# A hand-ordered selective scan: the order of GpSimd's products and of the sums behind them

## The chip, the cores and the metric

The kernel runs on one core of a Trainium2 chip. The metric is the device time of one execution in microseconds (us); of several executions the median is given.

## The reference

Four layers work on an image batch x of shape (4, 64, 64, 96) in float32. Layer 0 is group norm, an input projection to 192 channels and a gate, a 3x3 convolution, and a selective scan with 16 states per channel in four directions. Layers 1 to 3 are a convolution, linear attention with a quantised feed-forward network, and a Fourier filter with a second feed-forward network. The part that matters here is the scan:

```python
def step(h, inp):
    u_t, dt_t, B_t, C_t = inp
    dA = jnp.exp(dt_t[..., None] * A)
    h = dA * h + (dt_t * u_t)[..., None] * B_t[:, None, :]
    y = jnp.sum(h * C_t[:, None, :], axis=-1)
    return (h, y)
```

It is run over the 4096 positions of each image by rows and by columns, and each of these forwards and backwards; the four results are added.

## The kernel before

**Phases and steps.** The scans go over 4 images and 24 groups of 8 channels. 8 channels times 16 states fill the 128 partitions. Each pair of image and group (a unit u) has two phases, n = 2u by rows and n = 2u + 1 by columns, 192 phases in all. The 4096 positions are four chunks q of 1024. A phase has 8 steps, each with one scan instruction on VectorE (DVE): steps 0 to 3 go forward over q = 0 to 3 (L1970), steps 4 to 7 go backward over q = 3 to 0 (L1977). Below, "step 9" of a phase is step 1 of the next.

**What each engine does in a phase.** ScalarE (ACT) makes the decay factors `pa` with an exponential (`decay`, L1669 by rows, L1675 by columns, two instructions there) into PSUM. `B` holds dt·u, multiplied by the replicated B_t on GpSimd (POOL) by `times_b` (L1653). For a column phase ACT copies it in turned order into the single tile `Bc` (`copy_b`, L1628). The forward scan writes `S`. The backward scan writes over `pa`, and DVE then adds that to `S` (L1988); for the chunks in `apart[n]` it writes over `B` or `Bc` instead, and forward and backward results stay apart. POOL multiplies each result by the replicated C_t (`times_c`, L1658). TensorE (PE) sums over the 16 states (`reduce`, two blocks of a chunk, L1691) into the PSUM tile `py`, which collects a whole unit. ACT copies `py` to `ys` (`result`, L1698), and SyncE (SP) stores it.

**Two stages.** While images 1 to 3 are still being prepared (projection, convolution, softplus: the "pre" part of the main lane), only chunk 3 stays apart: three adds on DVE and five products on POOL per phase. When `done["pre"]` is set, chunks 2 and 3 stay apart: two adds, six products.

**The S tiles.** There are five. `places` says which tile chunk q of phase n takes: q = 1 takes the tile that q = 2 of the phase before had, q = 2 that of q = 3, q = 3 that of q = 1, and q = 0 that of q = 0 two phases before. A forward scan can start once the sum over the old content is done. `B` has four tiles: chunk q of the next unit takes the tile of chunk q ^ 1 of this one. `Bc` has one.

**What sets the order.** The part runs under a manual schedule, so each engine executes its instructions in the order in which the program issues them. `plan(n)` puts the loads, copies, products and sums of a phase at chosen steps with `at(t + k, ...)`, where t = 8n. After the instructions of a step, `pieces(step)` fills in side work: the "pre" part and layers 1 to 3 of images 0 to 2 (the main lane), and the gating and output projection behind the scans (the side lane). Side work is cut into pieces with a cost for each of PE, ACT, POOL, DVE and DMA; every step adds `gains[step]` to five credits (step counted to 16, a row and a column phase), a piece is issued when the credits cover it, and `cap` bounds what can be saved up. What is left over after the last scan is issued in the tail, before the last layers of image 3.

Of the kernel before, what the change touches and what calls it, by code (L numbers as in the profile page):

```python
# [73 lines left out]
def layers(ctx: ExitStack, tc: tile.TileContext, a: dict, out):  # L74
# [37 lines left out]
    late = []  # L112
# [22 lines left out]
    done = {}  # L135
# [1446 lines left out]
    def phase(n):  # L1582

        b, g = units[n // 2]
        return b, g, n % 2
# [130 lines left out]
    class Lane:  # L1716
# [32 lines left out]
    credit = [0.0] * 5  # L1749

    gains = [
        (2.8, 1.2, 0.4, 0.8, 1.6), (2.8, 1.2, 0.4, 0.8, 1.6),
        (2.8, 0.2, 0.4, 0.8, 1.6), (2.8, 0.4, 2.2, 0.8, 1.6),
        (2.8, 1.2, 0, 0.8, 1.6), (2.8, 1.4, 0.4, 0.8, 1.6),
        (3.2, 1.0, 1.2, 1, 1.8), (3.2, 2.4, 1.4, 1, 1.8),
        (2.8, 1.4, 0.4, 0.8, 1.6), (2.8, 1.4, 0.4, 0.8, 1.6),
        (2.8, 1.4, 0.4, 0.8, 1.6), (2.8, 2.4, 0.6, 0.8, 1.6),
        (2.8, 2.8, 0.6, 0.8, 1.6), (2.8, 1.4, 0.6, 0.8, 1.6),
        (3.2, 2.4, 0.8, 1, 1.8), (3.2, 2.4, 1.4, 1, 1.8),
    ]  # L1760
    cap = (4.4, 3.0, 3.2, 1.6, 4.0)

    def pieces(step):

        clock[0] += 1
        assert clock[0] % 16 == (step + 1) % 16
        for free, bank in returned:
            free.append(bank)
        returned.clear()
        for e in range(5):  # L1770

            more = 1.25 if e in (2, 4) and clock[0] > 8 * (N - NG) else 1
            credit[e] = min(cap[e], credit[e] + gains[step][e] * more)
        for lane in list(lanes):
            if not lane.live():
                lanes.remove(lane)
                continue
            for s in list(lane.streams):
                while s[1] is not None:
                    if s[1] == NEXT:  # L1780
                        if s[2] == clock[0]:
                            break
                        lane.advance(s)
                        continue
                    if s[1] == LONG:
                        if step != 12:
                            break
                        cost = (0, 5.0, 0, 0)
                    else:
                        cost = s[1]  # L1790
                        if any(
                            c > 0 and credit[e] < min(c, cap[e]) - 0.5 for e, c in enumerate(cost)
                        ):
                            break
                    for e in range(len(cost)):
                        credit[e] -= cost[e]
                    lane.advance(s)
                if s[1] is None:
                    lane.streams.remove(s)
# [88 lines left out]
    def at(step, f, *args):  # L1888
        acts.setdefault(step, []).append((f, args))

    def plan(n):

        t, u = 8 * n, n // 2
        two = "pre" in done
        apart[n] = (3, 2) if two else (3,)
        row = n % 2 == 0
        b, g, _ = phase(n)
        last, first = g == NG - 1, g == 0

        if row:  # L1900
            for q, k in ((0, 7), (1, 8), (2, 9), (3, 10)):
                at(t + k, load_du, u + 1, q)
            for q, k in ((0, 3), (1, 5), (2, 15), (3, 16)):
                at(t + k, load_delta, u + 1, q)
            if last:
                for q in range(NCH):
                    at(t + 2 + q, load_rep, b + 1, 0, q)
                for q, k in ((3, 8), (2, 9), (1, 11), (0, 12)):
                    at(t + k, load_rep, b + 1, 1, q)
            for q, k in ((2, 2), (3, 3), (1, 4), (0, 6)):  # L1910
                at(t + k, copy_b, u, q)
            if first:
                for q in range(NCH):
                    at(t + 6 + q // 2, copy_rep, b, q)
        else:
            for q, k in ((0, 2), (1, 3), (2, 6), (3, 9)):
                at(t + k, times_b, u + 1, q)

        if two:
            at(t + 4, times_c, n, 2)  # L1920
            at(t + 5, times_c, n, 3)
            at(t + 6, times_c, n, 3, True)
            at(t + 7, times_c, n, 2, True)
            at(t + 6, reduce, n, 2)
            at(t + 7, reduce, n, 3)
            at(t + 8, reduce, n, 3, True)
            at(t + 8, reduce, n, 2, True)
        else:
            at(t + 4, times_c, n, 3)
            at(t + 6, times_c, n, 3, True)  # L1930
            at(t + 7, times_c, n, 2)
            at(t + 6, reduce, n, 3)
            at(t + 8, reduce, n, 3, True)
            at(t + 8, reduce, n, 2)
        late = 0 if row else 1
        at(t + 8, times_c, n, 1)
        at(t + 9 + late, times_c, n, 0)
        at(t + 10, reduce, n, 1)
        at(t + 10 + 2 * late, reduce, n, 0)
        if not row:  # L1940
            at(t + 13, result, u)
            for j in range(4):
                at(t + 14 + j, store_result, u, j)

    with tc.manual_schedule():
# [4 lines left out]
        for step in range(8 * N):  # L1950
            n, k = divmod(step, 8)
            if k == 0:
                plan(n)
                if n % (2 * NG) == 2 * NG - 2 and n // 2 + 1 < len(units):
                    b = units[n // 2 + 1][0]
                    assert done.get(("back", b)) == NBLK, (n, done)
# [10 lines left out]
            if k < 4:  # L1967
                q = k
# [5 lines left out]
            else:  # L1974
                q = 7 - k
# [8 lines left out]
                else:  # L1984
                    if q:
                        edge = big.tile([128, 1], F32, tag="edge", name="edge", bufs=2)
                        nc.vector.tensor_copy(edge, to[:, 0:1])
                    nc.vector.tensor_tensor(Ss[n, q], Ss[n, q], to, ALU.add)  # L1988
            pieces(step % 16)
            if n == N - 1 and k >= 4:  # L1990
                for i in (2 * k - 8, 2 * k - 7):
# [24 lines left out]
def kernel_body(tc: tile.TileContext, a: dict, out):  # L2016
    layers(tc, a, out)
# [117 lines left out]
```

## Time and profile before

| | |
|---|---|
| median of 3 runs | 5522.77 us (5522.01 to 5528.18) |
| profiled execution | 5537.81 us |
| its span | 5536.0 us |
| busy PE / DVE / ACT / POOL | 77% / 83% / 64% / 72% of the span |
| scan 128x1024 on DVE | 2.28 us first of a row, 2.35 us others |
| product 128x1024 on POOL | 2.36 us, 1481 in all |
| add on DVE (L1988) | 1.22 us, 439 in all |
| copy into columns on ACT | 1.98 us, 384 in all |

The span is the time from the first to the last instruction in the trace; 1.8 us of the execution lie around it. The profiled execution is 15 us above the median of the others. The scans run from 299 to 5103 us. DVE's share counts only instructions, so a wait between two scans shows as idle time, and each row of the page says which engine's instruction ended it.

### The profile page before, as it was taken

The numbers are of one execution on the slowest core, as the hardware profiler recorded it, in microseconds if no ns is written. First come the engines' busy times: TensorE is split into PE (matmuls) and PEld (weight loads), VectorE is DVE, ScalarE is ACT, GpSimd is POOL, SyncE is SP. The second block draws the span as 40 slices with busy tenths as digits, with TensorE's granted clock in tenths as the row PEclk, the third lists the DMA queues.
The fourth block names the chain that finished last, engine by engine and source line by source line (L and its number), as shares of the span: only waits on it lengthen the run. The fifth ranks groups of instructions, "written<-read, shape, count | busy, mean of one in ns | idle before, by whom it ended". The sixth has DMA issues, their size and how long they took to land. (4 is left out here: it accounts for less than half of the span.)

```text
span 5536.0 us, 60837 instructions
## 1 busy us (share of the span) xinstructions
PE 4258.0 (77%) x20550; PEld 1581.5 (29%) x20550; DVE 4618.4 (83%) x3098; ACT 3566.0 (64%) x4554; POOL 3973.4 (72%) x1968
## 2 busy tenths in 40 slices
PE   7967888878886876777658876877578767786878
PEld 4422222222221221345102211542012213451346
DVE  4268888788889998999899999999898989998454
ACT  5667777777786568666865677576755676566133
POOL 1357877778778778878887788787987787787000
PEclk9977989888997986678668866787588768886888
DMA  4334444434456533455456434363565335563012
GB/s 125 91 110 115 126 114 117 135 105 124 117 162 175 163 99 89 128 160 156 125 145 173 117 87 119 115 200 103 147 170 146 97 99 165 161 176 96 17 55 96
DMA packets 298092, 694.68 MB, mean 125 GB/s; under 512 B 58184, under 2 KB 95156, under 8 KB 297652
## 3 DMA queue, kind: packets, MB, share of 16 engines
q1 hardware_dynamic: 297780, 690.80, 44.2%
q8 instruction: 162, 2.65, 0.2%
q14 instruction: 150, 1.23, 0.1%
HBM read 564.22 MB, written 126.35 MB: 125 GB/s over the span
## 5 line engine op out<-in xcount | busy, mean ns | idle before, releaser
L1658 POOL TENSOR_TENSOR S<-S,rep 128x1024 f32<-128x1024 f32 x768 | 1806.5, 2362 | 678.9 <-DVE S L1970 628.4
L1691 PE MATMUL py<-S,red 128*32 128x512 f32 x3072 | 956.8, 782 | 380.9 <-POOL S L1658 273.1
L1675 ACT ACTIVATE pa<-dl,nega 128x512 f32<-128x512 f32 x1152 | 792.9, 689 | 579.0 <-DVE Bc L1977 295.3
L1669 ACT ACTIVATE pa<-dl,nega 128x1024 f32<-128x1024 f32 x576 | 642.2, 1115 | 515.7 <-DVE S L1988 239.5
L1653 POOL TENSOR_TENSOR B<-B,rep 128x1024 f32<-128x1024 f32 x384 | 903.0, 2360 | 14.7 <-DMA B<-du_s 14.7
L1970 DVE TENSOR_TENSOR_SCAN S<-pa,S,Bc 128x1024 f32<-128x1024 f32 x288 | 676.3, 2348 | 230.8 <-PE py L1691 161.2
L1970 DVE TENSOR_TENSOR_SCAN S<-pa,S,B 128x1024 f32<-128x1024 f32 x288 | 675.8, 2347 | 134.0 <-PE py L1691 46.3
L1628 ACT COPY Bc<-B 128x1024 f32<-128x1024 f32 x384 | 741.0, 1982 | 0.0
L1988 DVE TENSOR_TENSOR S<-S,pa 128x1024 f32<-128x1024 f32 x439 | 533.7, 1216 | 6.6
L393 PE MATMUL p_conv<-low,conv_w 128*96 128x512 f32 x864 | 421.7, 639 | 32.0 <-ACT u L405 29.4
L1658 POOL TENSOR_TENSOR B<-B,rep 128x1024 f32<-128x1024 f32 x164 | 388.0, 2370 | 75.1 <-DVE pa L1977 38.8
L1977 DVE TENSOR_TENSOR_SCAN B<-pa,B 128x1024 f32<-128x1024 f32 x164 | 379.1, 2312 | 48.2 <-ACT Bc L1628 41.9
L1658 POOL TENSOR_TENSOR Bc<-Bc,rep 128x1024 f32<-128x1024 f32 x165 | 387.0, 2361 | 5.3 <-DVE pa L1977 4.0
L1977 DVE TENSOR_TENSOR_SCAN Bc<-pa,Bc 128x1024 f32<-128x1024 f32 x165 | 381.8, 2314 | 4.7
L1691 PEld LDWEIGHTS py<-S,red 128*32 128x32 f32 x3072 | 118.7, 121 | 908.9 <-POOL S L1658 518.0
L1234 POOL CAST h<-y 128x1536 fp8e5<-128x1536 f16 x64 | 95.5, 1492 | 312.7 <-ACT y L869 301.3
L1977 DVE TENSOR_TENSOR_SCAN pa<-pa,edge,B 128x1024 f32<-128x1024 f32 x124 | 291.5, 2350 | 2.8 <-ACT pa L1669 2.8
L1977 DVE TENSOR_TENSOR_SCAN pa<-pa,edge,Bc 128x1024 f32<-128x1024 f32 x123 | 289.2, 2351 | 5.2 <-ACT pa L1675 5.2
L1691 PE MATMUL py<-Bc,red 128*32 128x512 f32 x660 | 200.0, 787 | 95.1 <-POOL Bc L1658 95.1
L393 PE MATMUL p_conv<-high,conv_w 64*96 64x512 f32 (+1 forms) x576 | 265.0, 597 | 0.0
L1056 PE MATMUL p_mean<-t,centre 96*96 96x512 f32 x256 | 174.3, 792 | 110.7 <-ACT sq L1048 31.8
L1970 DVE TENSOR_TENSOR_SCAN S<-pa,B 128x1024 f32<-128x1024 f32 x96 | 218.9, 2280 | 23.3 <-ACT pa L1669 23.3
(274 smaller groups left out, 7411.4 us busy)
## 6 DMA issues: line engine op xcount, KB each, us to landing
dl<-delta_s SPq DMA_DIRECT2D x770, 256.0 KB
B<-du_s SPq DMA_DIRECT2D x768, 256.0 KB
z_s<-z SPq DMA_DIRECT2D x48, 512.0 KB
zl<-z_s SPq DMA_DIRECT2D x64, 384.0 KB
side<-y_s SPq DMA_DIRECT2D x112, 192.0 KB
rep<-bc_s SPq DMA_DIRECT2D x64, 256.0 KB
tw<-in_dft SPq DMA_DIRECT2D x64, 256.0 KB
side<-in_xT SPq DMA_DIRECT2D x64, 192.0 KB
```

Source lines behind the costliest of these rows:

```text
L393: nc.tensor.matmul(p, lhsT=conv_w[: src.shape[0], k, oc * C : (oc + 1) * C], rhs=src[:, ky : ky + RPB, kx : kx + HW], start=(k == 0), stop ...
L1056: nc.tensor.matmul(pm, lhsT=centre, rhs=t[:, blk(i)], start=True, stop=True)
L1234: nc.gpsimd.tensor_copy(h, y, saturate=False)
L1628: nc.scalar.copy(dst.rearrange("p (w h) -> p h w", h=HW)[:, q * h : (q + 1) * h, :], src.rearrange("p (h w) -> p h w", w=HW),)
L1653: nc.gpsimd.tensor_tensor(Bs[u, q], Bs[u, q], reps[units[u][0], 0, q], ALU.mult)
L1658: nc.gpsimd.tensor_tensor(t, t, c_of(n, q), ALU.mult)
L1669: nc.scalar.activation(pa, dls[u, q // 2][:, at : at + CH], AF.Exp, scale=scale)
L1675: nc.scalar.activation(to[:, k * HW // 2 : (k + 1) * HW // 2, :], src[:, :, q * w : (q + 1) * w], AF.Exp, scale=scale,)
L1691: nc.tensor.matmul(py[32 * j : 32 * j + 32, :], lhsT=red[:, 24 - 8 * s : 56 - 8 * s], rhs=x[:, k * BLK : (k + 1) * BLK], start=s == 0 and ...
L1970: nc.vector.tensor_tensor_scan(s, pas[q], b_of(n, q), Ss[n, q - 1][:, CH - 1 : CH] if q else 0.0, ALU.mult, ALU.add,)
L1977: nc.vector.tensor_tensor_scan(to[:, ::-1], pas[q][:, ::-1], b_of(n, q)[:, ::-1], edge if q < 3 else 0.0, ALU.mult, ALU.add,)
L1988: nc.vector.tensor_tensor(Ss[n, q], Ss[n, q], to, ALU.add)
```

## The change

The change moves issue places; no instruction of the computation is added to a phase or removed from it.

- `plan`: products and sums now come from one list of (chunk, backward or not, step of the product, step of the sum). In the first stage the order on POOL was S3, backward 3, S2, S1, S0 at steps 4, 6, 7, 8, 9 (10 in a column phase) with the sums at 6, 8, 8, 10, 10 (12); it is now S3, S2, backward 3, S1, S0 at 4, 6, 7, 8, 9 (11) with the sums at 6, 7, 8, 9, 10 (12). In the second stage the products keep their steps, apart from S0 of a column phase (10 to 11); the sums of S3, backward 3 and S1 move from 7, 8, 10 to 6, 7, 9.
- `copy_b`: chunk 3 is copied at step 2 and chunk 2 at step 3, instead of the other way round.
- `times_b` of chunk 2 moves from step 6 to 5 of a column phase in the first stage.
- `gains`: other credits for POOL and ACT at the steps; in the first stage PE's are multiplied by 0.9, ACT's by 1.05 and POOL's by 1.25.

```diff
     gains = [
+        (2.8, 0.8, 0, 0.8, 1.6), (2.8, 0.6, 0, 0.8, 1.6),
+        (2.8, 0, 2.2, 0.8, 1.6), (2.8, 0, 0.4, 0.8, 1.6),
         (2.8, 1.2, 0.4, 0.8, 1.6), (2.8, 1.2, 0.4, 0.8, 1.6),
-        (2.8, 0.2, 0.4, 0.8, 1.6), (2.8, 0.4, 2.2, 0.8, 1.6),
-        (2.8, 1.2, 0, 0.8, 1.6), (2.8, 1.4, 0.4, 0.8, 1.6),
-        (3.2, 1.0, 1.2, 1, 1.8), (3.2, 2.4, 1.4, 1, 1.8),
-        (2.8, 1.4, 0.4, 0.8, 1.6), (2.8, 1.4, 0.4, 0.8, 1.6),
-        (2.8, 1.4, 0.4, 0.8, 1.6), (2.8, 2.4, 0.6, 0.8, 1.6),
-        (2.8, 2.8, 0.6, 0.8, 1.6), (2.8, 1.4, 0.6, 0.8, 1.6),
-        (3.2, 2.4, 0.8, 1, 1.8), (3.2, 2.4, 1.4, 1, 1.8),
+        (3.2, 1.0, 1.2, 1, 1.8), (3.2, 2.4, 1.2, 1, 1.8),
+        (2.8, 1.4, 0.2, 0.8, 1.6), (2.8, 1.4, 0.2, 0.8, 1.6),
+        (2.8, 1.4, 0.2, 0.8, 1.6), (2.8, 2.4, 0.2, 0.8, 1.6),
+        (2.8, 2.8, 0.2, 0.8, 1.6), (2.8, 1.4, 0.2, 0.8, 1.6),
+        (3.2, 2.4, 0.6, 1, 1.8), (3.2, 2.4, 1.2, 1, 1.8),
     ]
...
             more = 1.25 if e in (2, 4) and clock[0] > 8 * (N - NG) else 1
+            if "pre" not in done:
+                more = (0.9, 1.05, 1.25, 1, 1)[e]
...
-            for q, k in ((2, 2), (3, 3), (1, 4), (0, 6)):
+            for q, k in ((3, 2), (2, 3), (1, 4), (0, 6)):
                 at(t + k, copy_b, u, q)
...
-            for q, k in ((0, 2), (1, 3), (2, 6), (3, 9)):
+            for q, k in ((0, 2), (1, 3), (2, 6 if two else 5), (3, 9)):
                 at(t + k, times_b, u + 1, q)
 
         if two:
-            at(t + 4, times_c, n, 2)
-            at(t + 5, times_c, n, 3)
-            at(t + 6, times_c, n, 3, True)
-            at(t + 7, times_c, n, 2, True)
-            at(t + 6, reduce, n, 2)
-            at(t + 7, reduce, n, 3)
-            at(t + 8, reduce, n, 3, True)
-            at(t + 8, reduce, n, 2, True)
+            order = ((2, False, 4, 6), (3, False, 5, 6), (3, True, 6, 7), (2, True, 7, 8))
         else:
-            at(t + 4, times_c, n, 3)
-            at(t + 6, times_c, n, 3, True)
-            at(t + 7, times_c, n, 2)
-            at(t + 6, reduce, n, 3)
-            at(t + 8, reduce, n, 3, True)
-            at(t + 8, reduce, n, 2)
-        late = 0 if row else 1
-        at(t + 8, times_c, n, 1)
-        at(t + 9 + late, times_c, n, 0)
-        at(t + 10, reduce, n, 1)
-        at(t + 10 + 2 * late, reduce, n, 0)
+            order = ((3, False, 4, 6), (2, False, 6, 7), (3, True, 7, 8))
+        end = (0, False, 9, 10) if row else (0, False, 11, 12)
+        for q, back, k, r in (*order, (1, False, 8, 9), end):
+            at(t + k, times_c, n, q, back)
+            at(t + r, reduce, n, q, back)
```

## The prediction

> **What bounds the kernel now.** I first read the page's busy shares and slices: VectorE (DVE) is busiest, and the column DVE in the 40 slices goes from 7 or 8 to 9 about a third of the way in. So the scans are cut in two by the number of reverse scans that are kept apart. The page has 439 adds at L1988; 192 phases need two each and a first-stage phase a third, so 439 - 384 = 55 phases belong to the first stage (three adds, five POOL products), and 137 to the second (two adds, six products). I then asked the busy time in each stage (columns: stretch, its length, then PE, PEld, DVE, ACT, POOL busy, clock, DMA).
>
> ```profile
> 298.60:1774.00 1475.40, 1191.73 (x3054) 346.40 (x3054) 1224.95 (x720) 1100.17 (x1396) 1139.50 (x602) 0.85 0.45 126
> 1774.00:5103.00 3329.00, 2462.76 (x13412) 909.67 (x13410) 3092.07 (x1835) 2165.97 (x2689) 2706.96 (x1243) 0.77 0.48 135
> ```
>
> DVE is 83% busy in the first stage (idle 250 us) and 93% in the second (idle 237 us). A pair of phases takes 1475.4 / 27.5 = 53.7 us in the first stage; DVE's own rows give 2 x 2.28 + 6 x 2.35 + 2 x 2.31 + 6 x 2.35 for the scans, 6 x 1.22 for the adds and 4 x 0.16 for the edges, 45.3 us, and about 26 gaps of 0.04 us: 46.3 us. So 7 us of each pair are waits. The waits of DVE say for what, first in the stretch to 1740 us, then 1740 to 4400 us (us, times, longest):
>
> ```profile
> DVE S L1970 <- PE py L1691: 150.1, 33, 7.5
> DVE B L1977 <- ACT Bc L1628: 14.6, 16, 1.1
> ...
> DVE S L1970 <- PE py L1691: 39.8, 25, 4.3
> DVE S L1970 <- ACT pa L1675: 21.8, 24, 2.6
> DVE B L1977 <- ACT Bc L1628: 18.4, 19, 2.6
> ```
>
> A forward scan waits for the sum over states (PE, L1691) that frees its S tile. Counting scans through DVE's timeline places the first-stage waits: 115.1 us in 21 waits at step 1 of a column phase (S of q=1, whose tile held q=2 of the row phase before), 9.4 us at step 1 of a row phase, 36 us at step 3 of both (the tile of the last phase's q=1). One of the 21, in the timelines of DVE, POOL and PE (start, us, operation; idle before it in brackets):
>
> ```profile
> 1302.51 2.28 DVE L1970 TENSOR_TENSOR_SCAN S<-pa,Bc 128x1024 f32<-128x1024 f32 x1
> 1312.32 4.80 DVE L1970 TENSOR_TENSOR_SCAN S<-pa,S,Bc 128x1024 f32<-128x1024 f32 x2 [7.53 <-PE py L1691]
> ...
> 1297.85 2.36 POOL L1658 TENSOR_TENSOR S<-S,rep 128x1024 f32<-128x1024 f32 x1
> ...
> 1294.76 8.43 PE L393 MATMUL p_conv<-low,conv_w 128*96 128x512 f32 x12 [1.27 <-ACT u L405]
> 1303.12 1.05 PE L1691 MATMUL py<-S,red 128*32 128x512 f32 x4
> 1304.10 1.09 PE L544 MATMUL p_dt<-xd,dt_w 6*96 6x512 f32 x2
> 1305.12 2.82 PE L393 MATMUL p_conv<-low,conv_w 128*96 128x512 f32 x6
> 1307.78 0.70 PE L330 MATMUL p_xp<-xb,w_twice 96*128 96x320 f32 x2
> ```
>
> The last line's operation is followed by more convolution; the sum of q=2 begins at 1311.00, beside the backward sum. The product had ended at 1300.2: the scan does not wait for work that is late, but for a sum that is queued behind others on PE.
>
> **What the skill says.** The Trainium skill, "PSUM — Partial Sum Buffer", section "Engine vs sequencer instructions", has ACT, DVE and POOL as strict FIFOs and matmuls in program order; the 10.8 us between that product and its sum agree. So where a sum stands in PE's order decides. "SBUF — State Buffer", section "Who interferes with whom", has a DVE instruction with two SBUF inputs contend with POOL's reads. The adds and scans here read one side from PSUM (pa), and POOL's products last 2362 ns on average, those on the tile B between 2.33 and 2.53 us; I price no contention for their new order. "TensorE: Matmul & The Clock Gate", section "What's actually happening", lets PE's clock follow how busy it was. The trace has 0.85 where PE is 81% busy and 0.77 where it is 74%; I price no change of clock.
>
> **The change part by part.**
>
> (1) Order of products and sums, first stage. The sum of q=2 stood at step 8, after the backward sum; it now stands at step 7, before it, and its product at 6 instead of 7. Its scan is at step 9, so there are two steps instead of one. From the two programs' orders on PE: between the sum of q=0 and this one stood on average 5.0 other matmuls, the sum of q=3, 6.6 more, and the backward sum; now 2.8, the sum of q=3 and 4.3. That is 4.5 matmuls fewer (each has two records; 12 records in the 7 to 8.4 us of a convolution give 1.2 us each), 5.4 us, and one sum of 1.05 us: 6.5 us sooner. The 21 waits average 5.5 us, the longest 7.5: about 110 of 115 us go, and all 9 us of row step 1. Moving the sum of q=1 from step 10 to 9 takes about half of the 36 us at step 3: 18. The POOL step of q=2 comes right after DVE's add at step 5, which is in time; what is behind it on POOL are the backward product and the softplus operations, which had idle before them.
>
> (2) The copies into columns (L1628) take q=3 first; the reverse scan of q=3 at step 4 then waits for the first copy, not the second. The copy is 1.98 us and the waits are 0.9 us: 15 us in the first stage, and most of the 26 us in the second. The scan of q=2 one step later then waits for the second copy, which has a step of 2.3 us to spare.
>
> Together 110 + 9 + 18 + 15 = 152 us of DVE's waits, 5.5 us per pair, to 48.2. **What is late next** is PE. It is busy 1191.7 / 27.5 = 43.3 us of each pair and idle 10.3. Its work is the same in kind and amount (17.9 matmuls of others per pair before, 17.5 after). Its idle time waits mostly for ACT's evacuations: 192 us are named to 1740 us, 7.7 per pair. With DVE faster some of this closes. If half of the 10.3 stays, a pair takes 48.5; if all 7.7 stay, 51.0. I take 6.2: 49.5, or 4.1 us less per pair, 27.5 x 4.1 = **-114 us**.
>
> (3) Second stage. Each phase's sums of q=3, backward q=3 and q=1 stand one step earlier. The waits on sums are 40 + 7 us up to the end, of which I take 30 (one more step is 2.3 us, the mean wait 1.6), and 18 of the copies' 18 + 8. A third comes back as waits on the decays on ACT (the row of 21.8): **-32 us**. Ends: -48, and plus what the rival below gives.
>
> (4) The planner's credits. PE's are cut to 0.9 in the first stage and ACT's raised to 1.05; POOL's are cut at the steps with a product. No instruction of the computation goes. The order of the changed program has 441 adds: the first stage has 57 phases. Two phases with one more add (1.22) and edge (0.16) each: **+3 us**. In the tail, about three blocks of the third image's last feed-forward are left over after the last scan: three plus three matmuls each, some 3 us of PE. A part falls into the 8.5 and 2.6 us for which PE waits for transfers there: **+6 us** (0 to 10).
>
> (5) One times_b (q=2, first stage) goes a step earlier, four steps after its load was issued instead of five. The load is a 256 KB transfer with over 9 us for it; POOL waited for such loads 14.7 us in the whole run. Nothing. The loads on SP keep their steps; the tile that the load at step 9 overwrites is still freed at step 8 or earlier. Nothing.
>
> Sum: -114 - 32 + 3 + 6 = -137. The profiled execution took 5537.8 us (span 5536.0), 15 us above the median of 5522.8; against its own time the sum gives 5401, against the median **5386 us**. About 0.2% (11 us) is what a measurement can tell from no change.
>
> **The rivals.**
> - PE becomes the bound of the first stage: all 7.7 us of waits on ACT stay and the second stage gives nothing. -73 + 9 = -64: 5459. For it: ACT is 75% busy and in order, and its copies stand in bursts at row steps 2 to 6, as before. Against it: ACT itself waits for DVE there (43 + 28 + 16 + 13 us from 600 to 1740 us).
> - All named waits go and nothing replaces them: -152 - 48 + 9 = -191: 5332. Against it: PE would have to be 90% busy (43.3 of 48.2 us).
> - Slower: sums a step earlier stop PE's queue. In the second stage PE already waits for POOL's products before a sum (186.0, 80.2 and 24.5 us for S, Bc and B from 1740 to 4400 us). A sum that stands nearer to its product holds the matmuls of the side work behind it; ACT, in order, then waits for those with the next decay behind. If DVE loses one decay (1.115 us) in each of 137 phases, +153: -114 + 9 + 153 = +48: 5571. It decides from (114 - 9) / 137 = 0.77 us per phase. Against it: PE is 26% idle there.
> - The change does not do what it says, for ACT's decays are as late as the sums, and each wait changes its name: 5523.
>
> **How the numbers follow.** Chances: the sum above 0.56 (its own range 5350 to 5430), PE bound 0.20, all waits gone 0.12, slower 0.08, names only 0.04. So faster 0.88, same 0.04, slower 0.08. From 5335 to 5480 leaves out about half of the third case, the slower one and the names: 2 in 10.
>
> **What would show it.** Right: 441 adds at L1988's place; the wait of the forward scans for py under 60 us in all; first-stage pairs near 49 to 50 us; PE busier than 85% there; the copies' wait under 15 us. Step (3) is wrong if DVE's waits on the decays grow by over 30 us; step (4) if the time from the last scan to the end grows by over 10 us. Wrong in all: waits for py remain at column step 1, or PE's idle per pair is still about 10 us.

## Result and profile after

The changed kernel takes 5563.74 us (median of 5 runs, 5551.78 to 5568.46) against 5528.18 us for the kernel before in the same session: ratio 1.0062, interval 1.0046 to 1.0078. It is slower, by 36 us, where 5386 us was forecast. The profiled execution took 5556.72 us, its span is 5554.8; the two spans differ by only 19 us, because the profiled execution of before lies above its median and that of after below.

The busy time in each stage of the changed kernel (columns as before: stretch, length, then PE, PEld, DVE, ACT, POOL busy, clock, DMA share, GB/s; the third line is the tail after the last scan):

```profile
290.60:1840.00 1549.40, 1312.19 (x3108) 365.31 (x3109) 1274.43 (x751) 1123.30 (x1420) 1173.03 (x616) 0.85 0.44 124
1840.00:5109.10 3269.10, 2448.60 (x13321) 907.63 (x13319) 3046.52 (x1802) 2131.92 (x2637) 2663.04 (x1223) 0.77 0.49 135
5109.10:5554.80 445.70, 358.14 (x3307) 200.54 (x3305) 218.68 (x328) 126.42 (x217) 52.76 (x54) 0.85 0.19 61
```

The page has 441 adds, so 57 phases are in the first stage and 135 in the second. A first-stage pair takes 1549.4 / 28.5 = 54.4 us; it took 53.7 and was to take 49.5. PE is busy 1312.2 / 28.5 = 46.0 us of it (43.3 before) and idle 8.3 (10.3 before). Each number of a stage here and below comes from one profiled execution. Such an execution lies up to 15 us from the median of its kernel, so differences between stages of that size decide nothing by themselves. The second stage takes 24.22 us per phase (24.31 before), the tail 445.7 us (430.4).

The spans' 19 us: the first scan starts 8 us earlier, in code that is the same in both. The first stage is 73 us longer. Two more phases at the second stage's pace account for 48.6; the other 24.6 are the slower pace. The second stage is 62 us shorter, 13 us more than its two missing phases. The tail is 15 us longer.

The waits of DVE, first stage and then second stage (us, times, longest):

```profile
DVE S L1959 <- PE py L1691: 86.5, 31, 4.6
DVE S L1959 <- ACT pa L1669: 75.8, 44, 23.2
DVE pa L1966 <- ACT pa L1675: 38.1, 19, 4.0
DVE S L1959 <- ACT pa L1675: 30.8, 20, 3.9
```

```profile
DVE S L1959 <- ACT pa L1675: 34.7, 39, 3.9
DVE pa L1966 <- ACT pa L1669: 27.5, 22, 2.6
...
DVE S L1959 <- PE py L1691: 5.6, 6, 2.1
```

The wait for sums did fall: from 160 to 86 us over the whole first stage, from 47 to 6 in the second. The copies into columns no longer stand among the first rows. But the decays on ACT stand in their place: their first-stage rows L1669 and L1675 for S were 25.8 and 7.0 us in the same stretch before (23 us of the first is the first scan in both kernels). Here is the place that the prediction showed, a column phase's step 1, in the changed kernel, on PE and then on DVE:

```profile
1443.63 1.92 PE L1691 MATMUL py<-S,red 128*32 128x512 f32 x4 [6.21 <-ACT ys L1698]
1445.48 2.02 PE L544 MATMUL p_dt<-xd,dt_w 6*96 6x512 f32 x2
1448.01 8.05 PE L393 MATMUL p_conv<-low,conv_w 128*96 128x512 f32 x12 [0.51 <-ACT u L405]
1455.99 1.05 PE L1691 MATMUL py<-S,red 128*32 128x512 f32 x4
1456.97 2.82 PE L393 MATMUL p_conv<-low,conv_w 128*96 128x512 f32 x6
1459.71 1.05 PE L1691 MATMUL py<-B,red 128*32 128x512 f32 x4
```

```profile
1457.26 4.80 DVE L1959 TENSOR_TENSOR_SCAN S<-pa,S,Bc 128x1024 f32<-128x1024 f32 x2 [4.02 <-PE py L1691]
```

The sum that frees the tile (1455.99) still comes 4 us late, although it now stands before the backward sum. PE stood still for 6.2 us ahead of it, waiting for ACT's copy of `py`, and then its matmuls took almost twice their time: 1.92 us for a sum that elsewhere takes 1.05, 2.02 us for a p_dt that elsewhere takes 1.09. Each sum now stands by itself. Before, two sums often stood side by side. In the timeline of the kernel before, the place of the prediction goes on so:

```profile
1310.99 0.62 PE L1691 MATMUL py<-B,red 128*32 128x512 f32 x2
1311.00 0.62 PE L1691 MATMUL py<-S,red 128*32 128x512 f32 x2
1311.44 0.60 PE L1691 MATMUL py<-B,red 128*32 128x512 f32 x2
1311.45 0.60 PE L1691 MATMUL py<-S,red 128*32 128x512 f32 x2
...
1314.73 1.06 PE L1691 MATMUL py<-S,red 128*32 128x512 f32 x8
```

Two sums in a row overlap in time: 8 records in 1.06 us, as long as 4 take alone. A sum is two matmuls, and each writes 32 of the 128 partitions of `py`: those of q = 0 and q = 2 the lower half, those of q = 1 and q = 3 the upper. Neighbours that write different halves run together. Neighbours that write the same half do not, as a forward and a backward sum of q = 3 in the second stage show (14 of the 15 such pairs in the kernel before run one after the other):

```profile
2135.07 1.05 PE L1691 MATMUL py<-S,red 128*32 128x512 f32 x4
2135.95 1.03 PE L1691 MATMUL py<-Bc,red 128*32 128x512 f32 x4
```

The Trainium skill, "TensorE: Matmul & The Clock Gate", Part 3, "Packing small matmuls — row/col tiling", describes how matmuls in different 32x32 tiles of the array run at the same time. Here two sums do so only when they stand next to each other in PE's queue. The new order took the neighbours apart. In PE's program order of the first stage, 95 of 275 sums stood directly behind another sum; now 40 of 285 do. Below, such a sum is said to have a neighbour. PE's time in sums (columns: stretch, length, PE, PEld, clock, DMA share, GB/s), before and then after:

```profile
298.60:1774.80 1476.20, 246.29 (x1096) 31.51 (x1096) 0.85 0.45 126
```

```profile
290.60:1840.00 1549.40, 347.33 (x1132) 43.80 (x1132) 0.85 0.44 124
```

That is 9.0 us of PE per pair before and 12.2 after, for the same sums; the clock is 0.85 in both.

### The profile page after: what moved, and what is told of

Read it like the earlier page. It is cut to its first block, busy times and chain, and to the rows that moved or that the text cites. A ratio compares the mean times of both kernels' runs of the same rounds, so it can differ in the third digit from the quotient of the medians.

```text
span 5554.8 us, 60794 instructions
## 1 busy us (share of the span) xinstructions
PE 4365.4 (79%) x20542; PEld 1597.5 (29%) x20542; DVE 4634.1 (83%) x3114; ACT 3563.4 (64%) x4542; POOL 3971.1 (71%) x1966
## 5 line engine op out<-in xcount | busy, mean ns | idle before, releaser
L1675 ACT ACTIVATE pa<-dl,nega 128x512 f32<-128x512 f32 x1152 | 791.1, 689 | 530.6 <-DVE Bc L1966 268.0
L1669 ACT ACTIVATE pa<-dl,nega 128x1024 f32<-128x1024 f32 x576 | 641.9, 1115 | 456.8 <-DVE S L1977 221.9
L1628 ACT COPY Bc<-B 128x1024 f32<-128x1024 f32 x384 | 747.7, 2009 | 16.2 <-POOL B L1653 11.9
L1691 PE MATMUL py<-Bc,red 128*32 128x512 f32 x656 | 231.5, 809 | 104.1 <-POOL Bc L1658 104.0
L1691 PE MATMUL py<-B,red 128*32 128x512 f32 x652 | 204.9, 709 | 61.8 <-POOL B L1658 61.8
L1966 DVE TENSOR_TENSOR_SCAN pa<-pa,B 128x1024 f32<-128x1024 f32 x96 | 226.1, 2356 | 26.3 <-ACT pa L1669 22.6
```

The source lines that it names most:

```text
L1628: nc.scalar.copy(dst.rearrange("p (w h) -> p h w", h=HW)[:, q * h : (q + 1) * h, :], src.rearrange("p (h w) -> p h w", w=HW),)
L1669: nc.scalar.activation(pa, dls[u, q // 2][:, at : at + CH], AF.Exp, scale=scale)
L1675: nc.scalar.activation(to[:, k * HW // 2 : (k + 1) * HW // 2, :], src[:, :, q * w : (q + 1) * w], AF.Exp, scale=scale,)
L1691: nc.tensor.matmul(py[32 * j : 32 * j + 32, :], lhsT=red[:, 24 - 8 * s : 56 - 8 * s], rhs=x[:, k * BLK : (k + 1) * BLK], start=s == 0 and ...
L1966: nc.vector.tensor_tensor_scan(to[:, ::-1], pas[q][:, ::-1], b_of(n, q)[:, ::-1], edge if q < 3 else 0.0, ALU.mult, ALU.add,)
```

## The experiments

Theory A: the sums' lost neighbours make PE's work larger, and that takes back what the slack gives. Theory B: the credits do it, by where side work stands. Theory C: the slack is worth nothing, because another wait follows close behind. (From e9 on the expectations also call it theory C that PE's queue paces the first stage.) The first stage of most of the kernels, per pair ("neighbours": sums directly behind another sum; "sums": PE's time in them):

| kernel | ratio [95%] | phases | pair us | PE busy / idle | sums | neighbours |
|---|---|---|---|---|---|---|
| before | 1 | 55 | 53.7 | 43.3 / 10.3 | 9.0 | 95 |
| after | 1.0062 [1.0046, 1.0078] | 57 | 54.4 | 46.0 / 8.3 | 12.2 | 40 |
| e1 order only | 1.0074 [1.0061, 1.0086] | 55 | 54.4 | 45.3 / 9.1 | 11.1 | 41 |
| e2 credits only | 1.0043 [1.0029, 1.0056] | 57 | 54.4 | 43.9 / 10.5 | 8.9 | 129 |
| e3 joined | 1.0015 [1.0008, 1.0021] | 57 | 53.0 | 43.6 / 9.5 | 9.9 | 77 |
| e4 split | 1.0034 [1.0023, 1.0045] | 55 | 54.5 | 44.3 / 10.2 | 9.7 | 72 |
| e5 joined, two | 0.9993 [0.9984, 1.0001] | 57 | 53.3 | 42.9 / 10.4 | 9.1 | 100 |
| e6 paired | 1.0010 [1.0002, 1.0019] | 55 | 53.5 | 44.0 / 9.5 | 9.5 | 93 |
| e9 before, light | 0.9877 [0.9863, 0.9890] | 55 | 51.4 | 40.9 / 10.5 | 9.7 | 95 |
| e10 after, light | 0.9845 [0.9831, 0.9858] | 57 | 50.6 | 41.6 / 8.9 | 12.2 | 40 |
| e11 paired, light | 0.9881 [0.9866, 0.9896] | 55 | 51.0 | 40.7 / 10.3 | 10.0 | 93 |
| e12 joined, three | 1.0046 [1.0033, 1.0059] | 57 | 54.3 | 42.6 / 11.7 | 8.5 | 124 |
| e13 joined, old credits | 0.9994 [0.9986, 1.0002] | 55 | 53.0 | 43.8 / 9.1 | 9.6 | 87 |
| e14 factors only | 0.9886 [0.9873, 0.9899] | 53 | 51.3 | 43.5 / 7.8 | 10.5 | 130 |
| e15 table only | 1.0068 [1.0056, 1.0080] | 65 | 53.8 | 41.1 / 12.7 | 9.9 | 147 |
| e17 after, old table | 0.9882 [0.9862, 0.9901] | 53 | 50.5 | 43.4 / 7.2 | 11.2 | 96 |
| e18 joined, factors | 0.9839 [0.9821, 0.9857] | 53 | 50.3 | 43.1 / 7.2 | 10.3 | 126 |

**The change in two halves.** e1 is the kernel before with the new order (all hunks of `plan` and `copy_b`), e2 with the new credits (all hunks of `gains` and `pieces`).

> The new order of products, sums and copies with the old credits (gains table and factors of the kernel before). Theory A, lost overlap: in the first stage 95 of 275 sums stood directly behind another sum in PE's order and ran beside it, now 41 do; each sum that runs alone costs PE about 1 us more, and PE is the second bound of the stage. Then the sums' PE time in the first stage is 335 to 345 us (247 before) and the time is still no better than before, 5535 to 5550 us, with the tail after the last scan as before. Theory B, the credits are at fault (side work spread differently, more of it left for the tail): without them the gain of the forecast appears, under 5480 us.

> The old order with the new credits alone. Theory A: the sums keep their neighbours (129 of 285 directly behind another), their PE time in the first stage stays near 250 us, and only the longer tail (about +19 us) and two more first-stage phases (+3 us) cost: 5535 to 5552 us. Theory B: the credits carry the whole loss and hide a gain of the order, so alone they cost over 50 us: above 5580 us.

Measured: 1.0074 (5572.6 us) and 1.0043 (5557.0 us); both cost, and both a little more than theory A had said. With the order alone PE's sums rise from 246 to 305 us (335 were expected at least) and the stage from 1476 to 1496. The waits of DVE in its first stage:

```profile
DVE S L1957 <- ACT pa L1675: 101.3, 36, 5.4
DVE S L1957 <- ACT lg L559: 64.8, 13, 6.0
DVE S L1957 <- ACT pa L1669: 47.9, 22, 23.3
DVE S L1957 <- PE py L1691: 24.7, 10, 6.2
```

So the waits for sums fell by 136 us, from 160 to 25, and the time rose: the scans wait for decays and for `lg`, the logarithm of the softplus on ACT, instead. With the credits alone the sums per pair do not rise; the stage has two more phases and a slower pace, and its granted clock is 0.81. Neither half alone is a gain, and theory B's times (under 5480 us for e1, above 5580 for e2) are missed by both.

**Neighbours put together, and taken apart.** e3 is the changed kernel with one number changed, so that the first stage's sum of q=3 stands at the step of that of q=2; e4 is the kernel before with one sum moved away from its neighbour.

```diff
-            order = ((3, False, 4, 6), (2, False, 6, 7), (3, True, 7, 8))
+            order = ((3, False, 4, 7), (2, False, 6, 7), (3, True, 7, 8))
```

```diff
-        at(t + 10 + 2 * late, reduce, n, 0)
+        at(t + (11 if row and not two else 10 + 2 * late), reduce, n, 0)
```

> The changed kernel with one number changed: in the first stage the sum of q = 3 stands at step 7 instead of 6, directly ahead of the sum of q = 2 (they write different 32-column parts of py). Its tile is not needed before step 10. Theory A: 77 instead of 40 of 285 sums have a neighbour, the sums' PE time in the first stage falls by about 37 x 1.05 = 39 us from 345, and the time by 20 to 39 us, to 5525 to 5545. Theory B, or PE's stall of 6.2 us per pair behind the copy of py as the cause: the stall stands ahead of the same sum, 5560 to 5568 us.

> The kernel before with one number changed: in the first stage the sum of q = 0 of a row phase stands at step 11 instead of 10, so that it no longer directly follows the sum of q = 1. Its tile is not needed before step 16. Theory A: 72 instead of 95 sums have a neighbour, their PE time in the first stage grows by about 23 us from 247, and the time by 10 to 24 us, to 5538 to 5552. Theory B and any cause in a wait of the scans: no scan waits for this sum, so 5525 to 5531 us.

Measured: 1.0015 and 1.0034. PE's time in sums, in e3 and then in e4:

```profile
296.10:1807.80 1511.70, 283.43 (x1132) 36.87 (x1132) 0.85 0.44 127
```

```profile
292.30:1791.80 1499.50, 265.51 (x1096) 34.34 (x1096) 0.85 0.44 124
```

One sum moved by one step gives 0.5% back in the changed kernel, and costs 0.3% in the kernel before, where PE has 19 us more in sums and the stage is 23 us longer. No scan needed that sum earlier in e4. Both times lie in the ranges of theory A: neighbours are worth PE's time, and that time counts.

**More neighbours.** e5 is e3 with the row sum of q=1 at step 10 beside that of q=0 (`(1, False, 8, 10 if row and not two else 9)`). e12 is e5 with the column's sums of q=1 and q=0 both at step 10, the product of q=0 at 9, `py` copied at 11 and the old order of copies. e16 is e5 with the old order of copies alone.

> e3 with one more number changed: in the first stage the sum of q = 1 of a row phase stands at step 10 instead of 9, directly ahead of the sum of q = 0. Theory A: 100 instead of 77 of 285 sums have a neighbour, the sums' PE time falls by some 24 us from 283, the time by 10 to 24 us against e3: ratio to the kernel before 0.997 to 1.000. Rival (slack is what counts): the scan at step 11 has one step again instead of two and waits for this sum; ratio 1.003 or more.

> A version to beat both: e5 with the copies in the old order and, in the first stage, the sums of q = 1 and q = 0 side by side in column phases too (step 10, with the copy of py at 11). 124 of 285 sums have a neighbour (100 in e5): some 25 us less of PE; theory A gives 10 to 25 us against e5: ratio 0.995 to 0.998. If more neighbours give nothing more: 0.999 to 1.001.

> e5 with the copies into columns in the old order; tells which of the two edits made e12 lose 0.5% against e5. If the copies: ratio 1.003 to 1.005, like e12. If the sums side by side in column phases with the early copy of py: 0.998 to 1.000, like e5, and it may be the fastest.

Measured: 0.9993, 1.0046 and 1.0000 [0.9991, 1.0008]. The row pair helps, as theory A had it. e12 lies outside both of its ranges: the column pair with the early copy of `py` costs, although sums fall to 8.5 us per pair, for PE's idle time rises to 11.7. The order of the copies is not the reason (e16). Why PE waits more in e12 stays open.

**Slack with the sums kept in pairs.** e6 is the kernel before with the new order of copies and this first stage (times_c and reduce: step); e7 adds the column's product of q=0 at 9, its sum at 10 and the copy of `py` at 11; e8 is the kernel before with the new order of copies alone.

```diff
-            at(t + 6, times_c, n, 3, True)
-            at(t + 7, times_c, n, 2)
-            at(t + 6, reduce, n, 3)
+            at(t + 6, times_c, n, 2)
+            at(t + 7, times_c, n, 3, True)
+            at(t + 7, reduce, n, 3)
+            at(t + 7, reduce, n, 2)
```

> The kernel before with its credits and its second stage; new are the order of the copies and, in the first stage, the products in the order S3, S2, backward 3 at steps 4, 6, 7, with the sums of q = 3 and q = 2 both at step 7 and the backward one at 8. So the sum of q = 2 has its second step of slack, and 93 sums (95 before) have a neighbour. If the lost neighbours alone ate the forecast gain, most of it appears now: ratio 0.980 to 0.990. If PE's own queue (its work and its stall behind the copy of py on ACT, 6.2 us per pair) is the bound of the stage, the scans' waits only change place: ratio 0.996 to 1.001.

> e6, and in the first stage the product and the sum of q = 0 of a column phase come at steps 9 and 10 (beside the sum of q = 1) instead of 10 and 12, and the copy of py on ACT at step 11 instead of 13, ahead of two of the three copies into columns. 117 sums have a neighbour. If PE's queue bounds the stage, its stall of about 6 us per pair behind that copy goes, and with it 60 to 120 us: ratio 0.978 to 0.990. If not, as e6, or slower where ACT now stops for the sum: ratio 0.997 to 1.005.

> The kernel before with only the order of the copies into columns changed. The forecast gave 15 us in the first stage and 18 in the second, less a third. If PE bounds the first stage, the 15 us there come back as waits for sums and only some 10 us of the second remain: ratio 0.997 to 1.000. If the waits simply go: 0.994 to 0.996.

Measured: 1.0010, 1.0009 [1.0000, 1.0018] and 1.0004 [0.9996, 1.0013]: no gain. The waits of DVE in the first stage of e6:

```profile
DVE S L1970 <- ACT pa L1675: 90.8, 31, 5.4
DVE S L1970 <- PE py L1691: 59.0, 14, 8.7
DVE S L1970 <- ACT lg L559: 45.3, 13, 4.5
```

101 us of waits for sums went (160 to 59). On the decays 84 us came (7 before), and 45 on `lg`. In e8 the 15 us of waits for the copies are gone from the first stage, and the waits for sums are 171 us there instead of 160. This is theory C, and with the old credits it is right. PE's own stalls stay. In the first stage PE waits for one evacuation on ACT in about every second pair (11 to 16 times), under a different name in each kernel: `p_z` for `sz` 85.3 us in the kernel before, `py` for `ys` 79.4 us in the changed one, `p_dt` for `sz` 70.5 us in e5, `p_z` for `sz` again 78.0 us in e7. That the decays are late because ACT, in order, stands behind matmuls which these stalls hold up is argued here, not shown.

**Less work on PE.** e9, e10 and e11 are the kernel before, the changed kernel and e6 with less convolution:

```diff
+                        if k in (3, 4, 5):
+                            continue
```

> The kernel before, leaving out 3 of the 15 matmuls of each convolution output of images 1 to 3 (144 of 720 in the first stage; the planner still counts them, so every other instruction keeps its place). Theory C, PE's queue paces the first stage: 144 x 1.2 us = 173 us of PE go, and the first stage falls from 1476 us by 100 to 170; ratio to the kernel before 0.970 to 0.982. Rival (ACT's order, or the scans' own waits for products, pace it): under 40 us, ratio above 0.993.

> The changed kernel with the same 3 of 15 convolution matmuls left out (images 1 to 3). Theory C: with PE relieved the lost neighbours cost less and the two steps of slack can show; first-stage pairs at 48 to 50 us, ratio to the kernel before 0.968 to 0.982, no more than 10 us from e9. If the lost neighbours are not a matter of PE's time but of waits of their own: still some 35 us slower than e9.

> e6 (neighbours kept, two steps of slack for the sum of q = 2, old credits) with the same matmuls left out. Theory C: against e9 the waits for sums at column step 1 fall further, and what slack is worth when PE is not the bound shows: 10 to 50 us faster than e9. Rival (slack is worth nothing at any load, for the decays on ACT are as late as the sums): within 8 us of e9.

Measured: 0.9877 [0.9863, 0.9890], 0.9845 [0.9831, 0.9858], 0.9881 [0.9866, 0.9896]. The first stage of e9, which answers to the first line of the prediction:

```profile
298.80:1711.80 1413.00, 1123.79 (x2762) 311.12 (x2764) 1225.69 (x721) 1098.74 (x1395) 1139.36 (x602) 0.80 0.46 131
```

And that of e10:

```profile
293.10:1733.90 1440.80, 1185.91 (x2821) 315.19 (x2822) 1273.61 (x750) 1124.62 (x1421) 1172.87 (x616) 0.84 0.47 133
```

PE is busy for 68, 126 and 89 us less than in the kernels that e9, e10 and e11 start from, and the stage is 63, 109 and 69 us shorter. So PE's queue, its work and its stalls in order, sets most of the first stage's pace. The gains are smaller than expected: e9's 63 us lie between theory C (100 at least) and its rival (under 40), and e10 is just outside its range. Part of the reason is a wrong price. A convolution's record lasts 0.59 us but overlaps the next one; the 1440 records of the kernel before keep PE busy for 682.5 us, 0.474 us each. By that the 288 left out had taken some 137 us, not 173. In e9 half of this came back, and the granted clock fell from 0.85 to 0.80; in e10 nearly all did, with 0.84 (0.85 in the changed kernel). With PE relieved, the changed kernel is the faster one (5448.5 against 5469.1 us). e11 is no faster than e9 (5473.5 us), as its rival said: more slack for one sum gave nothing there.

**The credits in two halves.** e14 is the kernel before with the three factors, e15 with the new table; e13 is e3 with all of the old credits.

```diff
+            if "pre" not in done:
+                more = (0.9, 1.05, 1.25, 1, 1)[e]
```

> e3 (new order, sums of q = 3 and q = 2 side by side) with the credits of the kernel before. If order and credits cost separately, taking the credits away gains what they cost in e2: ratio 0.996 to 0.999. If they depend on each other (e1 and e2 lose 0.7 and 0.4%, both together only 0.6%): 1.001 to 1.006, no better than e3.

> The kernel before with only the three factors of the first stage (PE 0.9, ACT 1.05, POOL 1.25) and the old table; first stage 53 phases. If the factors, which spread PE's side work, cost in e2: ratio 1.003 or more. If the table does: 0.998 to 1.001.

> The kernel before with only the new gains table; first stage 65 phases, ten more than before, each with one more add and edge on DVE (1.4 us). If PE's queue sets the first stage, its work per pair falls by 15% and the pair comes down to 48 to 50 us; what is left over for the tail grows by 40 to 70 us: ratio 1.000 to 1.010. If the table itself disturbs the order: above 1.015.

Measured: 0.9994, 0.9886 and 1.0068. For e14 no range was right, its gain was not foreseen, and e13 lies between its two. e15's ratio is in its range, but for other reasons: the pair stayed at 53.8 us and the tail grew by 15 us, where 48 to 50 and 40 to 70 were expected. The two halves of the credits pull against each other, and with the old credits no order tried gave as much as either. PE's waits in the first stage, from 300 us, in the kernel before, in e14 and in e15:

```profile
PE p_z L370 <- ACT sz L376: 85.3, 16, 5.6
```

```profile
PE py L1691 <- POOL S L1658: 120.1, 67, 11.5
```

```profile
PE p_xp L330 <- ACT low L338: 103.7, 14, 9.0
```

With the factors this stall on ACT is gone, and what is left are mostly short waits for products (1.8 us on average). With the table alone a longer one stands in its place. The table also gives POOL 8.8 credits in 16 steps instead of 11.6, and the side work of the first stage then needs 65 phases.

What such a stall costs is more than its length. One of them, in the timeline of the kernel before:

```profile
744.48 1.05 PE L1691 MATMUL py<-S,red 128*32 128x512 f32 x4
751.11 2.02 PE L370 MATMUL p_z<-xb,w_in 96*96 96x512 f32 x2 [5.57 <-ACT sz L376]
753.05 1.89 PE L1691 MATMUL py<-S,red 128*32 128x512 f32 x4
```

After 5.57 us of idle the next matmuls take almost twice their time. The granted clock, last but two in these lines, was 1.00 just before the stall and 0.53 behind it:

```profile
744.00:746.00 2.00, 1.53 (x6) 0.18 (x5) 1.89 (x2) 1.97 (x4) 1.59 (x1) 1.00 0.68 184
751.00:755.00 4.00, 3.83 (x6) 0.58 (x6) 3.96 (x2) 3.45 (x5) 3.63 (x3) 0.53 0.18 51
```

Over the first stage I took all groups that start within 8 us of the end of an idle time of 3.5 us or more: two matmuls of p_z take 2.02 us there (median) and 1.10 elsewhere, a sum 1.92 and 1.05. There are 34 such stalls in the kernel before, 31 after, 33 in e2, 37 in e15, and 12 in e14. These groups take some 93 us longer in the kernel before than the median of the same kind elsewhere in its stage, 101 us after, and 25 us in e14. The limit of 3.5 us is my choice; no run here tests it, and about a third of the kernel before's matmul records at half rate stand elsewhere. The Trainium skill, "TensorE: Matmul & The Clock Gate", section "HAM oscillation — how this bites in real kernels", tells of this: a wait longer than its window (the page gives about 3.4 us) puts PE back to half rate. The traces agree in what follows such a wait: 1.92 against 1.05 us, and a clock of 0.53. The first stage of e14 shows the clock:

```profile
298.30:1657.00 1358.70, 1153.24 (x2984) 338.50 (x2984) 1178.71 (x690) 1078.84 (x1372) 1106.54 (x588) 0.90 0.47 131
```

0.90, where the kernel before has 0.85.

**The table against the factors in the changed kernel.** e17 is the changed kernel with the old table and its own factors. e18 is the kernel before with the factors and e3's order.

> The changed kernel with the old table of credits; the three factors of the first stage (PE 0.9, ACT 1.05, POOL 1.25) stay, as do its order of sums, products and copies. The first stage has 53 phases, and 96 of its 265 sums stand directly behind another sum on PE. Theory 'the table is what costs in the changed kernel': the factors keep most of what they gave alone (0.9886), ratio to before 0.988 to 0.995. Rival 'the new order costs with any credits, as it did with the old ones (1.0074)': the order takes back what the factors give, ratio 0.995 to 1.004, and PE is busy 46 us or more per pair of the first stage against 43.5 with the factors alone.

> The kernel before with the three factors and, in place of its order, the new order with the first stage's sum of q=3 kept behind that of q=2 (products, sums and copies as in that experiment), with the old table. The first stage has 53 phases, and 126 of its 265 sums stand directly behind another sum. Theory 'slack before the scans adds to the factors where the sums keep their neighbours': ratio 0.980 to 0.987, pairs of the first stage under 51.0 us. Rival 'with the factors PE no longer makes the scans wait, so the order has nothing left to give': 0.987 to 0.990, pairs 51.0 to 51.6 us.

Measured: 0.9882 and 0.9839, both as the first theory had it. The table turns the changed kernel from a gain into a loss: without it the same order and factors are 1.2% faster than before. In e17 the order costs nothing against e14: with the old table and the factors 96 of 265 sums have a neighbour (41 of 275 in e1, which has neither factors nor table), PE is busy 43.4 us per pair, and the stalls stay few (11). e18 is 0.5% faster still than the factors alone, its first stage 25.7 us shorter. Its interval (0.9821 to 0.9857) does not meet that of e14. The DVE waits for sums in the first stage of e17 and of e18 (e14 has 95 us of them):

```profile
DVE S L1959 <- PE py L1691: 18.7, 23, 1.1
```

```profile
DVE S L1959 <- PE py L1691: 16.8, 19, 4.0
```

So the new order is worth about 26 us once PE stalls less and the sums keep their neighbours. How much of that is the slack before the scans, and how much the copies and the second stage, which e18 has from the new order too, was not taken apart. e18, 5442.76 us (5436.75 to 5451.32), is the fastest kernel here, 1.6% below the kernel before.

## Why the prediction was wrong

The change has three parts. All but one of their combinations were run (ratio to before):

| | old credits | factors | table | both |
|---|---|---|---|---|
| old order | 1 | 0.9886 | 1.0068 | 1.0043 |
| new order | 1.0074 | 0.9882 | not run | 1.0062 |

- **Step (1), the waits for sums: right in size by itself, and not a gain.** With the order alone (e1) they fell by 136 us in the first stage, where 137 was forecast, and the kernel became 0.7% slower. In the changed kernel they fell by 74, and 92 us were left in both stages where under 60 was to be; as e1 differs from it by the credits alone, these kept the rest. Stalls like the one shown are a part of it: 7 of the 31 waits, 26 of the 86 us, come within 18 us of a wait of PE for `ys`. What makes the others is open. Two readings in this step were off, and small: it counted the backward sum's 1.05 us as standing ahead of the sum of q = 2, which in its own words ran beside it, and it took 1.2 us for a matmul from a stretch partly at half rate (8.43 us for 12 records, at a mean clock of 0.62), where the 2.82 us for 6 records shown below it give 0.94.
- **Step (2), copies: nothing.** The wait went, but e8 gave 1.0004: waits for sums and decays grew instead.
- **"What is late next is PE. Its work is the same in kind and amount": this sentence failed, and with it the 6.2 us of idle time set beside it.** The count of matmuls was the same, their time was not. PE's busy time per pair was to stay 43.3 and became 46.0, for the sums lost their neighbours. e1 and e13 differ by the place of one sum, which gives the neighbours back: 1.0074 and 0.9994, some 44 us. PE's idle time was to fall to 6.2 and fell to 8.3; with the old credits and neighbours it is 9.1 (e13) and 9.5 (e6), and the forecast gain does not appear there either. It is lowest with the factors and the old table (7.8 in e14, 7.2 in e17 and e18). (2.7 + 2.1) x 27.5 = 132 us is the gap between the forecast of -114 us and the +19 us that 27.5 pairs lost in pace (the two extra phases lost 6 us more). The lines of the trace of before where two sums overlap were in view, and the prediction did not price what overlap is worth. The order alone, forecast at about -146 us with step (3), measured +41 (0.74% of 5530).
- **Step (4), credits: mis-sized, and the largest term.** They were priced by what they add, +9 us, and POOL's factor of 1.25 was left out of the reckoning. Together they cost +0.43%, some 24 us; apart, the factors give -63 us and the table costs +38 alone, and some +99 in the changed kernel (1.0062 against 0.9882). They decide where side work stands on PE, and so whether PE stalls. The changed kernel does not stall more than the kernel before (31 and 34 times); it lacks what the factors give with the old table (11 or 12 times). "I price no change of clock" was right for the mean, 0.85 again, but the mean hid stretches at half rate after stalls. The two extra phases were right (441 adds). The tail's +6 (0 to 10) was +15, which the prediction had named as a sign against this step.
- **Step (3), second stage: right in size of the waits, wrong in gain.** Waits for sums went from 47 to 6 us and the copies' from 26 to 2, and the waits on decays grew from 44 to 81, more than the 30 that were to show the step wrong: -13 us, not -32. And even that seems to come from the table: the kernels with the new table take 24.15 to 24.26 us per phase, with either order, those with the old one 24.25 to 24.48.
- **Step (5): nothing was seen against it.** The copies' row of ACT (L1628) has 11.9 us of idle for `times_b` in the whole run of the changed kernel, too little to decide anything.
- **The rivals.** The slower one (sums stop PE's queue in the second stage) did not occur there, so that the kernel did become slower, at a chance of 0.08, does not speak for it. "Each wait changes its name" describes e6 to e8. "PE becomes the bound" was nearest, but it had PE's work fixed. None had the side work's places as a cause.

Open: why e12 makes PE wait more, which of the three factors removes the stall, and how the table brings it back.

## What to carry to other kernels

Where side work is placed by credits, price a change of credits by the stalls it makes or removes on the in-order engine, not by the work it adds, and try its parts apart: here the table cost 0.7% alone and 1.8% in the changed kernel, and the factors gave 1.1%. Before a small matmul is moved for slack, look in the timeline whether it overlaps with a neighbour, and move both. A wait that goes is a gain only if no other stands close behind it: here 136 us of waits went with no gain at all. The TensorE stalls of 3.5 us and more seen here cost their length and then the half rate of what followed.

## What was not expected of the hardware

Sums of 128x32 by 512 columns in float32 that stand next to each other in PE's queue and write different halves of `py` run side by side: 8 records in 1.06 us against 4 in 1.05; with other matmuls between them they do not. Taking the same matmuls, some 137 us, from PE gave 68 us in e9, where the granted clock fell from 0.85 to 0.80, and 126 us in e10, where it fell from 0.85 to 0.84 only. With fewer stalls the clock was higher (0.90 in e14, 0.85 before).
